# Other engines for the transposes, the squares and the early loads in the first rows of a two-layer image kernel

## The chip, the cores and the metric

The kernel runs on one core of a Trainium2 chip. The metric is the time of one execution on the device, in microseconds (us). In the profile's short names PE is TensorE (PEld its weight loads), DVE is VectorE, ACT is ScalarE, POOL is GpSimd and SP is SyncE, which here only asks for DMAs.

## What is computed

The input is 32 images of 56 x 56 tokens with 128 channels, in fp32. Two residual layers follow one another:

```python
x = x + L0(_gn(x))    # window attention: 7x7 windows, rolled by 3, 4 heads, mask, bias table
x = x + L1(_gn(x))    # DCT along width and along height, 32 modes mixed, inverse DCT, feed-forward
```

`_gn` is a group normalization without weights: 32 groups of 4 channels, mean and variance over the image. In layer 0 each window of 49 tokens makes q, k and v, softmax over 49 keys with a position bias, the product with v and a projection. In layer 1 the first 32 DCT modes of each line are mixed over the channels, once along the width and once along the height, turned back and summed; then comes `relu(h @ W1 + b1) @ W2 + b2` with 512 hidden channels.

## The kernel before

The whole batch is one stream of cycles. A cycle takes in one row of windows (8 windows of 7 x 7 tokens, 392 tokens); an image has 8 such rows, so row r belongs to image r // 8. The work of a row is spread over five cycles, and layer 1 of an image follows from 11 cycles after its first row (`CONV_BEGIN` = 11) over the next 16 cycles. The order on TensorE, ScalarE, VectorE and GpSimd is written out by hand: under `manual_schedule` each of these engines executes its instructions in the order in which the Python code issues them. SyncE's queue is not part of that, and is ordered by the planner.

For row r the stages are:

- cycle r: `attn_q` and `attn_k` (TensorE, evicted by ScalarE), `attn_scores` (TensorE, then VectorE adds the bias and mask, L494), `attn_max` (VectorE takes the maximum, L504, GpSimd subtracts it, L505), `attn_v` (TensorE, copied by ScalarE, L471)
- cycle r or r + 1: `attn_exp` (ScalarE, L511)
- cycle r + 1: `attn_recip` (VectorE sums and inverts, L516 and L518) and `attn_divide` (GpSimd, six multiplications, L530). They write the quotients into `blocks`, cut up in such a way that a transpose of 32 x 32 blocks puts the whole tile right
- cycle r + 2: `attn_transpose` (VectorE, one transpose of 128 x 1024, L540) into `eT`; `load_tokens` asks for the residual input (`xr`)
- cycle r + 3: `add_bias` (GpSimd, L130, on `xr`), `attn_values` (TensorE, output and its bias into `oT` by VectorE, L587, and ScalarE, L589; with the argument `both` by ScalarE alone), `attn_project` (TensorE, then VectorE adds the residual into `x1`, L610; the result is also stored to DRAM)
- cycle r + 4: `attn_sums` (VectorE, L627), `attn_squares` (ScalarE, L639), `sum_squares` (VectorE, L643) and `add_sums` (GpSimd, L653), for the second normalization

Cycles 0 to 10 are written in `first_rows`. Later cycles follow `halves_first`, `eighths`, `quarters`, `behind_max`, `halves_last`. The scratch `a` of the softmax has three buffers in the first cycles and two later; the third is borrowed from a buffer of layer 1 (`xf`).

An image is read in four quarters (`load_quarter`: k is the upper or lower part of the rows, u the left or right half), each with four DMAs of 112 KB, and turned by VectorE (`turn_quarter`, L339 to L344). Image 0's quarters go into the two buffers `y`, which layer 1 first writes in cycle 11. All later images use one buffer `xin`, so a quarter is asked for only when the one before it has been turned. `next_steps` says in which cycle which quarter is turned: for image 1 in cycles 1, 2, 4 and 5, for image 2 from cycle 8 on. `norm_step` issues the first normalization of the next image in pieces.

The constants of layer 1 are asked for by SyncE (`back_weights`: inverse DCT; `ff_weights`: feed-forward), the mixing weights by ScalarE (`mix_weights`). The tag `hid` has four buffers of 128 x 512 for the hidden layer, which begins in cycle 19. TensorE writes into banks `pa0` to `pa3` in turn for the attention (`attn_bank`) and into four banks `pc` for layer 1 (`conv_bank`).

Of the kernel before, what the change touches and what calls it, by code (L numbers as in the profile page):

```python
# [9 lines left out]

F32 = mybir.dt.float32
AF = mybir.ActivationFunctionType
# [30 lines left out]
FF_AT = (8, 9, 10, 12, 13, 14, 15)  # L43
KB = 32
CONV_BEGIN = NWR + 3


@with_exitstack
def swin_fourier_kernel(
# [86 lines left out]

    def load_quarter(b, k, u):

        if b:
            t = work.tile([P, HW, KB], F32, tag="xin", name="xin", bufs=1)  # L140
        elif u:
            t = others[k]
        else:
            t = y_of[k][:, : S * KB].rearrange("p (w c) -> p w c", w=S)
            others.append(t[:, HW:])
            t = t[:, :HW]
        rows = slice(k * (S - KB), k * (S - KB) + KB)
        for cb in range(C // KB):
            cs = slice(cb * KB, (cb + 1) * KB)
            queue = nc.scalar if b == 0 and cb % 2 else nc.sync  # L150
            queue.dma_start(t[cs], x[b, rows, u * HW : (u + 1) * HW, cs])
        return t

    xins, others = {}, []
    for k in range(2):
        for u in range(2):
            xins[0, k, u] = load_quarter(0, k, u)
# [87 lines left out]
    idctw = const.tile([P, 2 * S], F32, tag="idctw", name="idctw")  # L245
    idcth = const.tile([P, S, 2], F32, tag="idcth", name="idcth")

    def back_weights(li):
        if li == 0:
            nc.gpsimd.memset(idctw, 0.0)  # L250
            nc.gpsimd.memset(idcth, 0.0)
        with nc.allow_non_contiguous_dma(reason="constant, once"):
            for blk in range(4 * li, 4 * li + 4):
                ls = slice(blk * NM // 2, (blk + 1) * NM // 2)
                modes = slice(blk // 2 * NM + blk % 2, (blk // 2 + 1) * NM, 2)
                nc.sync.dma_start(idctw[ls], idct_w[modes, li * 2 * S : (li + 1) * 2 * S])
                src = idct_h.rearrange("p (h r) -> p h r", r=4)[modes, :, 2 * li : 2 * li + 2]
                nc.sync.dma_start(idcth[ls, : S - SS], src[:, SS:])
                nc.sync.dma_start(idcth[ls, S - SS :], src[:, :SS])

    w1sb = const.tile([P, NM, C], F32, tag="w1sb", name="w1sb")
    w0sb = const.tile([P, NM, C], F32, tag="w0sb", name="w0sb")
# [10 lines left out]
    b2half = const.tile([P, JP], F32, tag="b2half", name="b2half")  # L273

    def ff_weights():
        nc.sync.dma_start(wff1, W1)
        nc.sync.dma_start(b1sb, b1.rearrange("(f p) -> p f", p=P))
        nc.sync.dma_start(wff2, W2.rearrange("(f p) o -> p f o", p=P))
        nc.sync.dma_start(b2sb, b2.partition_broadcast(P))
        for hs in HALVES:  # L280
            nc.sync.dma_start(b2half[hs], b2[hs].partition_broadcast(JP))

    mhalf = const.tile([P, 1], F32, tag="mhalf", name="mhalf")
    nc.gpsimd.memset(mhalf, -0.5)
# [6 lines left out]

    k_sb = big.tile([P, 2, NWR, WT], F32, tag="k", name="k")
    heads = const.tile([P, 2], F32, tag="heads", name="heads")
    nc.vector.memset(heads, 0.0)
# [2 lines left out]
    q_sb = big.tile([P, RT + JP - WT], F32, tag="q", name="q")  # L299
    nc.gpsimd.memset(q_sb, 0.0)  # L300
    v_sb = [big.tile([P, NP, C], F32, tag=f"v{i}", name=f"v{i}") for i in range(3)]
    a_sb = [big.tile([P, NH, NP, WT], F32, tag=f"a{i}", name=f"a{i}") for i in range(2)]

    def attn_buffer(r):
        return a_sb[r % 3 if r < CONV_BEGIN + 4 else r % 2]

    blocks = [
        big.tile([P, 2, NH * NP, KB], F32, tag=f"blocks{i}", name=f"blocks{i}") for i in range(2)
# [59 lines left out]
    def image_norm(im):  # L368

        GR = C // 16  # L370

        def average(out, src):
            sums = small.tile([P, GR], F32, tag="gsums", name="gsums", bufs=2)
            nc.vector.tensor_reduce(
                sums, src.rearrange("p (g c) -> p g c", c=4), axis=AX.X, op=ALU.add
            )
            nc.vector.tensor_scalar(
                out.rearrange("p (g c) -> p g c", c=4),
                sums.unsqueeze(2).to_broadcast([P, GR, 4]),
                0.25,  # L380
                None,
                ALU.mult,
            )

        nc.vector.bn_aggr(stat[:, 0:2], im.st)

        turned = small.tile([P, 32], F32, tag="turned", name="turned", bufs=2)
        nc.vector.transpose(turned, stat)
        mean = small.tile([P, 2, 32], F32, tag="gmeans", name="gmeans", bufs=1)
        average(mean[:, 0], turned)  # L390
        yield
        nc.vector.tensor_tensor(turned, turned, mean[:, 0], ALU.subtract)
        nc.vector.tensor_tensor(turned, turned, turned, ALU.mult)
        average(mean[:, 1], turned)
        back = small.tile([P, 2, 32], F32, tag="back", name="back", bufs=2)
        nc.vector.transpose(
            back.rearrange("p k c -> p (k c)"), mean.rearrange("p k c -> p (k c)")
        )
        gm = back[:, 0, 0:1]

        im.mean = small.tile([P, 1], F32, tag="mean0", name="mean0")
        nc.vector.tensor_scalar(im.mean, gm, -1.0, None, ALU.mult)

        ve = small.tile([P, 1], F32, tag="ve", name="ve")
        nc.vector.scalar_tensor_tensor(
            out=ve, in0=back[:, 0, 1:2], scalar=1e-5, in1=back[:, 1, 0:1], op0=ALU.add, op1=ALU.add
        )
        rstd = small.tile([P, 1], F32, tag="rstd0", name="rstd0")
        nc.gpsimd.tensor_tensor(rstd, ve, mhalf, ALU.pow)
        im.w = work.tile([P, 3 * C], F32, tag="wn", name="wn")  # L410
        im.bias = small.tile([P, 5], F32, tag="bqkv", name="bqkv")
        yield
        nb = small.tile([P, 1], F32, tag="nb0", name="nb0")
        nc.vector.scalar_tensor_tensor(
            out=nb, in0=gm, scalar=-1.0, in1=rstd, op0=ALU.mult, op1=ALU.mult
        )
        nc.scalar.mul(im.w, wqkv, rstd)  # L417
        yield
        pb = attn_bank()
        halved(pb[:, 0:1], wqkv[:, 2 * C :], nb)  # L420
        nc.vector.tensor_copy(im.bias[:, 2:3], pb[:, 0:1])
        yield
# [97 lines left out]

    def attn_divide(r, rs):
        a3 = attn_buffer(r).rearrange("p t w j -> p (t w) j")
        dst = blocks[r % 2]
        lo, hi = (slice(0, KB), slice(KB, JP)), (slice(JP, JP + KB), slice(JP + KB, P))
        halves = [(slice(0, P), slice(0, P), k, k) for k in range(2)]
        for a, b in (lo, hi):
            halves += [(a, b, 1, 0), (b, a, 0, 1)]
        for to, src, k, kb in halves:
            n = (KB, WT - KB)[kb]
            nc.gpsimd.tensor_tensor(  # L530
                dst[to, k, :, :n],
                a3[src, :, kb * KB : kb * KB + n],
                rs[src].unsqueeze(2).to_broadcast([src.stop - src.start, 2 * NWR, n]),
                ALU.mult,
            )

    def attn_transpose(im, i, r):

        eT = work.tile([P, NH * NP, JP], F32, tag="eT", name="eT")
        nc.vector.transpose(eT.rearrange("p t (k j) -> p k t j", k=2), blocks[r % 2])  # L540
        im.eT[i] = eT

# [91 lines left out]
    def attn_squares(im, i):  # L634
# [1 line left out]
        n0, n1 = WS * i // 2, WS * (i + 1) // 2  # L636
        piece = x1[:, n0:n1]
        im.sq = im.xr.pop(i)[:, : n1 - n0]
        nc.scalar.activation(im.sq, piece, AF.Square, scale=valid)  # L639

    def sum_squares(im, i):

# [331 lines left out]
    def halves_first(cycle):  # L974
# [15 lines left out]
        if im:  # L990
# [2 lines left out]
            attn_k(im, i)  # L993
            if i == NWR - 2:
                wrap_rows(cycle)
        if last and cycle > CONV_BEGIN and not behind_short:
            attn_squares(last, j)
            sum_squares(last, j)
        if not behind_short:
            next_tokens(cycle)  # L1000
        if cycle % NWR == 0:
            norm_step(cycle)
# [50 lines left out]
    def eighths(cycle):  # L1053
        im, i = row(cycle - 3)
        if im:
            attn_values(im, i, cycle - 3, cycle % NWR in VALUES_BY_ACT)
            if cycle % NWR == NWR - 1:
                attn_squares(*row(cycle - 4))
        for im, c in fourier(cycle):
            if c == 0:  # L1060
# [61 lines left out]
    def next_quarter(cycle):  # L1122
        b, quarter, late, _ = next_steps(cycle)
        if quarter:
            turn_quarter(images[b], *quarter)
        if late:
            xins[(b, *late)] = load_quarter(b, *late)

    def wrap_rows(cycle):
# [15 lines left out]

    EARLY = (0, 3, 4, 5, 7)
    VALUES_BY_ACT = (3, 6, 7)

    def halves_last(cycle):
        im, i = row(cycle)  # L1150
# [20 lines left out]
    def next_begin(cycle):  # L1171
        b, quarter, _, _ = next_steps(cycle + 1)
        if quarter:
            if quarter == (0, 0):
                images[b] = image_begin(b)
            xins[(b, *quarter)] = load_quarter(b, *quarter)

    def first_rows(cycle):  # L1180
# [12 lines left out]
        if cycle:  # L1193
            attn_exp(cycle - 1)
        if im3:
            attn_values(im3, i3, cycle - 3)
        tokens_bias(cycle)
        if im:
            attn_scores(im, i, cycle)
# [25 lines left out]
                norm_step(NWR - 1)  # L1225
        if 1 < cycle < 10:
            mix_weights(cycle - 2)
        if cycle in (6, 7):
            back_weights(cycle - 6)
        if cycle == 8:  # L1230
            ff_weights()
        if cycle == CONV_BEGIN - 1:
            attn_sums(im3, i3)
# [5 lines left out]
    with tc.manual_schedule(engines={ET.PE, ET.Activation, ET.DVE, ET.Pool}):  # L1239
        images[0] = image_begin(0)  # L1240
        for k in range(2):
            for u in range(2):
                turn_quarter(images[0], k, u)
            if k:
                copy_wrap(images[0], nc.vector.tensor_copy)
            for i in range(NP * k, NP * k + NP):
                row_stats(images[0], i)
        for _ in range(3):
# [2 lines left out]
            for half in range(2):  # L1251
                bias_and_mask(nc.vector, r, t, half)
        extra = big.tile([P, S, S], F32, tag="xf", name="a_extra", bufs=2)
        extra = extra.rearrange("p r w -> p (r w)")[:, : NH * NP * WT]
        extra = extra.rearrange("p (t w j) -> p t w j", t=NH, w=NP)
        a_sb.append(extra)
        for cycle in range(NB * NWR + CONV_BEGIN + FF_AT[-1] - NWR + 1):
            if cycle < CONV_BEGIN:
                first_rows(cycle)
# [27 lines left out]
                columns_turn(cycle, 0)  # L1287
            columns_turn(cycle, 1)
            last_fetch(cycle)
            if cycle % NWR == NWR - 1 and row(cycle - 4)[0]:  # L1290
                sum_squares(*row(cycle - 4))
                next_tokens(cycle)
            behind_max(cycle)
# [64 lines left out]
```

## Time and profile before

| | |
|---|---|
| time, median of 3 runs | 3254.74 us (3251.01 to 3256.28) |
| the profiled execution | 3245.75 us, its span 3244.0 us |
| TensorE busy | 3136.1 us (97%) |
| VectorE busy | 2538.4 us (78%) |
| GpSimd busy | 2343.1 us (72%) |
| ScalarE busy | 2165.5 us (67%) |
| mean TensorE clock | 0.988 of full |

Busy times are of the whole span. The span can be cut into slices or windows, and each then shows its own share for every engine; matmuls are pipelined and their ends are modelled. A wait is shown beside the instruction that waited, with the instruction that released it. Times in the views count from the start of the span.

### The profile page before, as it was taken

Reading aid. Unit: us, or ns where it says so; the run is one execution under the profiler, and the core shown is the slowest. Engines: PE = TensorE matmul, PEld = TensorE weight load, DVE = VectorE, ACT = ScalarE, POOL = GpSimd, SP = SyncE. Lnnn points to the kernel's source line nnn. Section 1 sums busy time; section 2 is a strip of 40 time slices with the busy share of each in tenths; the row PEclk is TensorE's granted clock in tenths of the full one; section 3 lists DMA queues with packets and bytes.
Section 4 is the critical chain, followed back from the end, with each engine's and each line's share of the span. In section 5 each row is a group of like instructions: output and inputs, shape, how many; then the busy total and the mean of one; then the engine's idle time right before and its main releaser. Section 6 shows DMA issues by size and latency. Waiting matters only on the chain. (4 is left out here: it accounts for less than half of the span.)

```text
span 3244.0 us, 151708 instructions
## 1 busy us (share of the span) xinstructions
PE 3136.1 (97%) x65664; PEld 2363.2 (73%) x65664; DVE 2538.4 (78%) x4787; ACT 2165.5 (67%) x3959; POOL 2343.1 (72%) x2634
## 2 busy tenths in 40 slices
PE   5689999999999999999999999999999999999999
PEld 3467777777777777777777777777777777777776
DVE  8778887878887878888888887878888877887741
ACT  3466776666777666667676776666776666677663
POOL 7777777777777777777777777777777777777741
PEclk8789999999999999999999999999999999999999
DMA  6545556655566656566656556655666656565453
GB/s 113 111 116 147 142 139 145 137 142 139 140 146 146 141 142 144 134 143 148 142 140 147 139 142 145 140 141 144 142 141 148 138 145 144 134 145 139 119 143 96
DMA packets 1173439, 448.46 MB, mean 138 GB/s; under 512 B 529482, under 2 KB 1142908, under 8 KB 1172772
## 3 DMA queue, kind: packets, MB, share of 16 engines
q1 hardware_dynamic: 1163428, 433.22, 56.3%
q8 instruction: 516, 8.45, 1.1%
q10 hardware_dynamic: 8736, 5.38, 0.7%
q14 instruction: 151, 1.24, 0.1%
q0 software_dynamic: 608, 0.17, 0.0%
HBM read 277.00 MB, written 161.48 MB: 135 GB/s over the span
## 5 line engine op out<-in xcount | busy, mean ns | idle before, releaser
L530 POOL TENSOR_TENSOR blocks<-a,rs 128x512 f32<-128x512 f32 x1506 | 1280.0, 857 | 415.1 <-DVE rs L518 291.3
L116 PE MATMUL pc<-xf,wff 128*64 128x512 f32 (+2 forms) x3584 | 714.2, 539 | 1.8 <-DVE xf L820 1.6
L116 PE MATMUL pc<-wff,hid 128*64 128x128 f32 x12288 | 714.1, 273 | 1.7 <-ACT hid L847 1.0
L116 PEld LDWEIGHTS pc<-wff,hid 128*64 128x64 f32 x12288 | 680.4, 137 | 10.3 <-ACT hid L847 5.3
L505 POOL TENSOR_TENSOR a<-a,mx 128x784 f32<-128x784 f32 x251 | 377.7, 1505 | 285.6 <-DVE mx L504 270.2
L116 PEld LDWEIGHTS pc<-xf,wff 128*64 128x64 f32 x3584 | 266.0, 136 | 370.0 <-issue 274.8
L847 ACT ACTIVATE hid<-pc,b1sb 128x512 f32<-128x512 f32 (+2 forms) x896 | 500.5, 643 | 40.9 <-PE pc L116 40.8
L116 PE MATMUL pa<-xw,wn 128*64 128x392 f32 x2048 | 396.0, 501 | 29.8 <-ACT wn L417 29.8
L471 ACT COPY v<-pa 128x512 f32<-128x512 f32 x256 | 151.9, 593 | 349.1 <-PE pa L464 346.2
L494 DVE TENSOR_TENSOR a<-pa,bm 128x392 f32<-128x392 f32 x502 | 260.0, 559 | 152.8 <-PE pa L486 141.6
L451 ACT ACTIVATE k<-pa,bqkv,heads 128x392 f32<-128x392 f32 x512 | 318.9, 674 | 14.7 <-PE pa L116 0.6
L540 DVE STREAM_TRANSPOSE eT<-blocks 128x1024 f32<-128x1024 f32 x256 | 314.2, 1227 | 0.9 <-POOL blocks L530 0.9
L852 POOL TENSOR_TENSOR res<-res,b2sb 128x512 f32<-128x512 f32 (+1 forms) x224 | 252.7, 1128 | 85.1 <-DMA res<-scr 70.8
L438 ACT ACTIVATE q<-pa,bqkv 128x392 f32<-128x392 f32 x256 | 149.8, 585 | 242.6 <-PE pa L116 240.9
L130 POOL TENSOR_TENSOR xr<-xr,bproj 128x384 f32<-128x384 f32 (+1 forms) x256 | 293.0, 1144 | 25.0 <-DMA xr<-in_x_dram 10.5
L738 ACT ACTIVATE y<-modes,rstd 128x448 f32<-128x448 f32 x256 | 276.6, 1137 | 42.9 <-DVE modes L731 31.9
L464 PE MATMUL pa<-wn,xw 128*64 128x128 f32 x4096 | 291.2, 284 | 7.1 <-issue 3.3
L511 ACT ACTIVATE a<-a 128x784 f32<-128x784 f32 x251 | 214.7, 856 | 118.4 <-POOL a L505 118.3
L557 PEld LDWEIGHTS pa<-eT,v 49*32 49x32 f32 x16384 | 173.1, 106 | 161.1 <-issue 63.9
L516 DVE TENSOR_REDUCE sm<-a 128x16 f32<-128x784 f32 x251 | 241.3, 961 | 54.9 <-ACT a L511 54.1
L602 PE MATMUL pa<-wproj,oT 128*64 128x128 f32 x3584 | 246.4, 276 | 20.7 <-DVE oT L587 20.5
L464 PEld LDWEIGHTS pa<-wn,xw 128*64 128x64 f32 x4096 | 227.5, 140 | 45.5 <-ACT oT L589 8.1
(112 smaller groups left out, 4915.1 us busy)
## 6 DMA issues: line engine op xcount, KB each, us to landing
zscr<-z SPq DMA_DIRECT2D x512, 112.0 KB
xin<-in_x_dram SPq DMA_DIRECT2D x496, 112.0 KB
htok<-scr SPq DMA_DIRECT2D x256, 196.0 KB
zT<-zscr SPq DMA_DIRECT2D x192, 256.0 KB
res<-scr SPq DMA_DIRECT2D x160, 256.0 KB
out_dram<-res SPq DMA_DIRECT2D x160, 256.0 KB
scr<-x SPq DMA_DIRECT2D x256, 112.0 KB
xr<-in_x_dram SPq DMA_DIRECT2D x256, 84.0 KB
```

Of the source, the lines that this page charges most:

```text
L116: nc.tensor.matmul(dst[ps], lhsT=lhsT[:, ps], rhs=rhs, start=start, stop=stop)
L130: nc.gpsimd.tensor_tensor(piece, piece, bproj.unsqueeze(1).to_broadcast([P, n, C]), ALU.add)
L451: nc.scalar.activation(k_sb[:, u], pk[:, :RT].rearrange("p (w j) -> p w j", j=WT), AF.Identity, bias=im.bias[:, 3 + u : 4 + u], scale=head ...
L464: nc.tensor.matmul(pv[HALVES[w % 2], w // 2 * C : (w // 2 + 1) * C], lhsT=im.half[i // NP][:, t0 : t0 + JP], rhs=im.w[:, 2 * C : 3 * C], s ...
L494: nc.vector.tensor_tensor(a[:, 2 * hp : 2 * hp + 2, :, 0:WT].rearrange("p u w j -> p w u j"), ps[hp][:, :RT].rearrange("p (w u j) -> p w u ...
L505: nc.gpsimd.tensor_tensor(a3, a3, mx.unsqueeze(2).to_broadcast([P, 2 * NWR, WT]), ALU.subtract)
L530: nc.gpsimd.tensor_tensor(dst[to, k, :, :n], a3[src, :, kb * KB : kb * KB + n], rs[src].unsqueeze(2).to_broadcast([src.stop - src.start, 2 ...
L540: nc.vector.transpose(eT.rearrange("p t (k j) -> p k t j", k=2), blocks[r % 2])
L602: nc.tensor.matmul(pp[hs, (n - n0) * C : (n - n0 + 1) * C], lhsT=oT[:, t0 : t0 + JP], rhs=wproj, start=True, stop=True,)
L738: nc.scalar.mul(y[:, r], t.rearrange("p (n k) -> p n k", k=NM), im.rstd)
L847: nc.scalar.activation(hf[:, :n], ph[:, :n], AF.Relu, bias=b1sb[:, f : f + 1])
L852: nc.gpsimd.tensor_tensor(im.res[:, :k], im.res[:, :k], b2sb.unsqueeze(1).to_broadcast([P, k, C]), ALU.add,)
```

## The change

For the first 16 rows (images 0 and 1) the softmax quotient is formed in place by one GpSimd multiplication, and TensorE transposes it by 32 matmuls against an identity, in two `pc` banks that ScalarE copies into `eT`. The `a` buffers get a tail of 15 zeros so that a 64 column slice of the last window stays inside, and keep their rotation over three until row 17. In `first_rows` the values are evicted by ScalarE alone. The squares of the first 11 rows are made by GpSimd in a `hid` buffer. Image 1's quarters go into the `y` buffers too, each asked for once image 0's quarter there has been turned. The constants of layer 1 are asked for by ScalarE, in smaller portions for the inverse DCT. In all images, squares and token loads of the cycle with i = 6 now stand as late as those of i = 7.

```diff
+TURNED_BY_PE = 2 * NWR
     def load_quarter(b, k, u):
-        if b:
+        if b > 1:
             t = work.tile([P, HW, KB], F32, tag="xin", name="xin", bufs=1)
-        elif u:
-            t = others[k]
         else:
             t = y_of[k][:, : S * KB].rearrange("p (w c) -> p w c", w=S)
-            others.append(t[:, HW:])
-            t = t[:, :HW]
+            t = t[:, u * HW : (u + 1) * HW]
...
-    def back_weights(li):
-        if li == 0:
-            nc.gpsimd.memset(idctw, 0.0)
-            nc.gpsimd.memset(idcth, 0.0)
+    nc.gpsimd.memset(idctw, 0.0)
+    nc.gpsimd.memset(idcth, 0.0)
+
+    def back_weights(blk):
+        li = blk // 4
...
-                nc.sync.dma_start(idctw[ls], idct_w[modes, li * 2 * S : (li + 1) * 2 * S])
...
+            nc.scalar.dma_start(idctw[ls], idct_w[modes, li * 2 * S : (li + 1) * 2 * S])
...
     def ff_weights():
-        nc.sync.dma_start(wff1, W1)
...
+        nc.scalar.dma_start(wff1, W1)
...
+    ident = work.tile([P, HB], F32, tag="hid", name="ident", bufs=NF)[:, :P]
+    make_identity(nc, ident)
...
-        turned = small.tile([P, 32], F32, tag="turned", name="turned", bufs=2)
+        turned = small.tile([P, 32], F32, tag="turned", name="turned", bufs=1)
...
     def attn_divide(r, rs):
         a3 = attn_buffer(r).rearrange("p t w j -> p (t w) j")
+        if r < TURNED_BY_PE:
+            nc.gpsimd.tensor_tensor(
+                a3, a3, rs.unsqueeze(2).to_broadcast([P, 2 * NWR, WT]), ALU.mult
+            )
+            return
...
     def attn_transpose(im, i, r):
         eT = work.tile([P, NH * NP, JP], F32, tag="eT", name="eT")
+        if r < TURNED_BY_PE:
+            a2 = a_ends[r % 3]
+            for g in range(0, NH * NP, NWR):
+                pt = conv_bank()
+                for k in range(NWR):
+                    for u, hs in enumerate(HALVES):
+                        nc.tensor.matmul(
+                            pt[u * JP : (u + 1) * JP, k * WT : (k + 1) * WT],
+                            lhsT=a2[:, (g + k) * WT : (g + k) * WT + JP],
+                            rhs=ident[:, u * JP : u * JP + WT],
+                            start=True,
+                            stop=True,
+                        )
+                nc.scalar.copy(
+                    eT[:, g : g + NWR, :WT], pt[:, :RT].rearrange("p (k j) -> p k j", j=WT)
+                )
+            im.eT[i] = eT
+            return
...
     def attn_squares(im, i):
...
-        nc.scalar.activation(im.sq, piece, AF.Square, scale=valid)
+        if NWR * im.b + i < CONV_BEGIN:
+            im.sq = work.tile([P, HB], F32, tag="hid", name="sq", bufs=NF)
+            im.sq = im.sq.rearrange("p (n c) -> p n c", c=C)[:, : n1 - n0]
+            nc.gpsimd.tensor_tensor(im.sq, piece, piece, ALU.mult)
+        else:
+            nc.scalar.activation(im.sq, piece, AF.Square, scale=valid)
...
     # halves_first
-        if last and cycle > CONV_BEGIN and not behind_short:
+        late = im and i in LATE_SQUARES
+        if last and cycle > CONV_BEGIN and not late:
             attn_squares(last, j)
             sum_squares(last, j)
-        if not behind_short:
+        if not late:
             next_tokens(cycle)
...
     # eighths
-            if cycle % NWR == NWR - 1:
+            if row(cycle)[0] and cycle % NWR in LATE_SQUARES:
                 attn_squares(*row(cycle - 4))
...
+    LATE_SQUARES = (6, 7)
...
     # first_rows
-            attn_values(im3, i3, cycle - 3)
+            attn_values(im3, i3, cycle - 3, True)
...
         if 1 < cycle < 10:
             mix_weights(cycle - 2)
-        if cycle in (6, 7):
-            back_weights(cycle - 6)
-        if cycle == 8:
+            back_weights(cycle - 2)
+        if cycle == 10:
             ff_weights()
...
     # start
             if k:
                 copy_wrap(images[0], nc.vector.tensor_copy)
+            for u in range(2):
+                xins[1, k, u] = load_quarter(1, k, u)
...
     # behind last_fetch(cycle)
-            if cycle % NWR == NWR - 1 and row(cycle - 4)[0]:
+            if row(cycle)[0] and cycle % NWR in LATE_SQUARES:
                 sum_squares(*row(cycle - 4))
                 next_tokens(cycle)
```

## The prediction

> **What bounds the kernel now.** I read the span in slices first, then windows of 50 us, then the waits and the instructions in order of time from 25 to 235 us. The change touches only that stretch, apart from one move of the squares.
>
> ```profile
> PE   5689999999999999999999999999999999999999
> ...
> DVE  8778887878887878888888887878888877887741
> ...
> POOL 7777777777777777777777777777777777777741
> PEclk8789999999999999999999999999999999999999
> ```
>
> TensorE (PE) is full from the fourth slice on; each slice is 81 us. Only the first three have room. By windows:
>
> ```profile
> 50.00:100.00 50.00, 33.47 (x680) 25.08 (x680) 42.80 (x88) 21.57 (x40) 42.33 (x50) 0.77 0.54 124
> 100.00:150.00 50.00, 32.80 (x642) 23.96 (x643) 40.63 (x76) 21.46 (x37) 38.27 (x44) 0.75 0.47 107
> 150.00:200.00 50.00, 35.60 (x784) 27.57 (x780) 40.52 (x73) 31.46 (x60) 34.10 (x39) 0.86 0.54 123
> 200.00:250.00 50.00, 45.17 (x896) 32.16 (x896) 40.17 (x76) 31.44 (x54) 38.25 (x43) 0.90 0.55 123
> 250.00:300.00 50.00, 49.93 (x1098) 38.89 (x1096) 40.21 (x76) 34.07 (x67) 37.54 (x42) 1.00 0.56 141
> ```
>
> The columns are TensorE, its weight loads, VectorE, ScalarE, GpSimd, clock, DMA share, GB/s. From about 220 us TensorE is busy throughout, at full clock: from row 24 to 32, and from 32 to 40, q starts 96.5 us apart, so 12.06 us a cycle. Whatever is won before 220 us should be kept to the end; nothing can be won after it.
>
> In cycles 4 to 10 (56 to 129 us, 10.5 us each) VectorE and GpSimd share the bound. One cycle, row 5:
>
> ```profile
> 67.23 1.02 DVE L494 TENSOR_TENSOR a_extra<-pa,bm 128x392 f32<-128x392 f32 x2
> ...
> 68.28 0.97 DVE L504 TENSOR_REDUCE mx<-a_extra 128x16 f32<-128x784 f32 x1
> ...
> 69.17 0.68 DVE L643 TENSOR_REDUCE part<-xr 128x32 f32<-128x512 f32 x1
> 69.33 1.50 POOL L505 TENSOR_TENSOR a_extra<-a_extra,mx 128x784 f32<-128x784 f32 x1
> 69.76 0.96 DVE L516 TENSOR_REDUCE sm<-a 128x16 f32<-128x784 f32 x1
> ...
> 70.93 1.19 DVE L540 STREAM_TRANSPOSE eT<-blocks 128x1024 f32<-128x1024 f32 x1
> ...
> 71.15 5.34 POOL L530 TENSOR_TENSOR blocks<-a,rs 128x512 f32<-128x512 f32 x6
> ...
> 72.04 0.52 DVE L610 TENSOR_TENSOR x<-pa,xr 128x384 f32<-128x384 f32 x1
> ```
>
> VectorE runs without a gap, and the sum of the squares (L643) follows the maximum at once, because ScalarE had squared long before. TensorE waits for VectorE, which in turn waits for the input:
>
> ```profile
> PE pa L602 <- DVE oT L587: 19.4, 6, 6.3
> DVE xw L339 <- DMA xin<-in_x_dram: 8.4, 2, 5.7
> ```
>
> In cycles 11 to 17 (11.5 us each) a serial loop decides: project add, values, transform, scores, score add, maximum, subtract, exp, sum, reciprocal, next project add. At cycle 12 it runs 0.63, 1.03, 1.87, 1.58, 1.04, 0.97, 1.50, 0.86, 0.97, 0.25: 10.7 us.
>
> **What the Trainium skill says.** (1) "SBUF — State Buffer", Who interferes with whom: a VectorE instruction with two SBUF inputs contends with a GpSimd one that reads SBUF, and the loser blocks fully. The trace agrees: the 128x32 product at L393 took 0.19 us at 21.61 and 1.07 here, under the divide:
>
> ```profile
> 84.61 1.07 DVE L393 TENSOR_TENSOR turned<-turned 128x32 f32<-128x32 f32 x1
> ```
>
> (2) "TensorE: Matmul & The Clock Gate", Part 1: an idle window (about 3.4 us) halves the clock. It agrees: after waits of 4 to 6 us the 32 score matmuls take 1.58 us, otherwise 0.90. (3) "GPSIMD Engine Reference", 3.1: two-input work costs about 2.6 cycles an element. The bias add at L130 gives (1.27-1.00)/128 = 2.1 ns an element. (4) "DMA: Bandwidth & Descriptors", Issuing engines are not separate DMA queues: another issuer saves only issue time. No run here shows that yet; the issues are 0.33 to 0.5 us on either queue.
>
> **The change part by part** (a minus is a gain).
>
> *Image 1 preloaded, 16 DMAs on SP.* The DMA share was 0.74 at 20 to 30 us and 0.01 at 30 to 40. One quarter (0.45 MB) was already there; 1.35 MB more at the 115 GB/s of the first 20 us is 12 us, and the first quarter is used at 39.6. The start I take as 0; if the loads hold up wqkv or the bias table (VectorE begins on it at 23.77, and had 2.2 us to spare before row 0) it is +3. Since xin stays free, image 2's first quarter no longer waits:
>
> ```profile
> 100.80 1.09 DVE L339 STREAM_TRANSPOSE xw<-xin 128x512 f32<-128x512 f32 x1 [5.69 <-DMA xin<-in_x_dram]
> ```
>
> Its last piece was issued at 97.28, behind SP's waits and the first idct constants. That is -5.7. The next quarter is asked for when the first is turned and takes about 7 us; VectorE has 7 us of work there by the sum below, so of 2.7 us I take -2.2.
>
> *Constants on ScalarE.* Three idct DMAs with one of mix_weights in each of cycles 2 to 9, six ff DMAs at cycle 10: 4 x 0.43 = 1.7 us of ScalarE's sequencer ahead of the next q. ScalarE is 43% busy (21.57 of 50), VectorE's stage is longer: 0, or +0.6 a cycle where the cover fails. SP's 24 idct issues (87.8 to 103.8) go; that gain is counted above.
>
> *Cycles 0 to 3.* No squares yet. The divide of row 0 (5.35 us, ending 45.36) held up its transpose, the values and row 3's scores, and xin cost 1.75. Now one product like L505 (1.5 us) ends at 41.6; TensorE transposes at 41.7 to 43.6, copies follow. Carried to row 4's score add: 56.2 for 59.13. **-3.0.**
>
> *The transpose on TensorE.* 32 matmuls with 128x64 weights and 49 columns. The nearest is L464: 16 in 1.09 us, weights in 0.85. So 1.7 to 2.2 us at full clock, up to 3.9 at half (16 took 1.95). Two ScalarE copies of 128x392 at 0.59. In cycles 4 to 10 TensorE then has 7.2 us at full clock a cycle, under VectorE's.
>
> *Cycles 4 to 10 on VectorE.* From score add to the end of project add it took 5.3 us. The transpose goes (-1.1 of issue slot), and the output bias of the values (L587, -0.6). But the squares now stand on GpSimd behind the subtract, and VectorE's sum of squares stands directly behind the maximum: it waits 0.06 + 1.46 (subtract) + 1.14 (1.00 or 1.28, as L130) + 0.05 = 2.7 us. All that VectorE has behind it, the row sum, reciprocal and project add, waits too; GpSimd's product and TensorE's next values wait for those. Net +1.05 a cycle, x7 = **+7.4**; row 7's second squaring in cycle 10 has no maximum to hide in, +1.5. The bounds are -1.7 a cycle, if the wait falls in time that TensorE needs anyway, and +1.3. The norm step (82.62 to 86.84) no longer meets a 5.3 us divide: **-1.8**. Sum to cycle 10: -3.0-5.7-2.2+7.4+1.5-1.8 = **-3.8**.
>
> *Cycles 11 to 18.* In 11 the divide held row 11's subtract from 137.2 to 139.24: -1.7 (-0.2 if v's copy, now behind the transpose, comes first). In 12 that copy stands before the exp: +1.2 (0 to +1.7). In 14, where TensorE is full (8.8 of 10 us), the transpose costs +1.8. In 15 the divide held the subtract, and with it rstd and the new weights: -2.2. The transposes fill gaps of 4 to 6 us, and scores and inverse transforms run warm: five times 0.7, **-3.4**. Sum **-4.3**.
>
> *Late squares at row 6, all images.* VectorE's sum and the load of xr come some 5 us later; the bias add of the next cycle is behind the load on GpSimd, then the divide. TensorE's work covers that (22 us idle in 3000): 0, bounds -3 and +3. New memsets and the identity go into GpSimd's 5 us of waits before 23 us; spare SBUF and shared slots: 0.
>
> Total -3.8 - 4.3 = **-8**: 3245.75 (span 3244.0 and 1.75 around it) becomes 3237.7. The median of the runs is 9.0 above that execution, so 3246.7.
>
> **Rivals.** *A, clearly faster:* the wait on the squares lies in time that TensorE's order takes anyway, and only the shorter work counts: part of 1.7 x 7 = 12 us gained in place of 8.9 lost. Two thirds of that way is -14: about -22 in all, 3233. For it: VectorE and GpSimd were full at 60 to 90 us. Against: VectorE had no gap where it could wait.
>
> *B, slower:* the transposes run at half clock. TensorE's order from scores to scores is then 3.9 + 1.55 (project) + 1.95 (v) + 2.7 (q, k) + 0.6 + 1.58 = 12.3 us against some 10, in half of seven cycles +8; no -3.4; cycles 12 and 14 lose 2 more each, and the xr loads 2: +9 in all, 3264. For it: the clock of 0.75. It decides if the clock between 50 and 150 us stays under 0.77 although TensorE has more to do.
>
> *C, no effect:* the loop of cycles 11 to 17 contains neither divide nor transpose, and gives the lead back: 0, 3255.
>
> **Numbers.** The likeliest 0.40, A 0.25, B 0.25, C 0.10. A measurement here can tell about 0.2% (6.5 us). Of the likeliest, whose terms reach from -17 to +1, 0.26 lies beyond it and 0.14 within. Faster 0.51, same 0.24, slower 0.25. The range goes from A's -27 to B's +9: 3228 to 3264.
>
> **What would show it.** Right: VectorE's L643 waits about 2.7 us on GpSimd in cycles 4 to 10, no wait of 5.7 at L339, subtract right behind maximum in cycles 11 and 15, transposes of 1.7 to 2.2 us, clock over 0.85 from 50 to 150, TensorE full at about 212 us. Wrong: no such wait, or q of row 11 before 120 us (A); a clock under 0.77 (B); a cycle after 250 us that isn't 12.06.

## The result and the profile after

The changed kernel takes **3249.5 us** (median of 20 runs, 3244.9 to 3254.1), the kernel before 3254.5 in the same comparison (20 runs, 3249.4 to 3258.1): ratio 0.9984, interval 0.9978 to 0.9991, so 5 us less where 8 were forecast. The profiled execution took 3248.8 us, its span is 3247.0.

The number came out, but not by the reasons given. Against the profiled execution of before (3245.7, a quick one, 9 us under its median) the steady part, behind row 24, is 5 us shorter and the start is 8 us *longer*: row 24's q (ScalarE's copy of it out of the bank, as all q starts below) is at 290.0 us in place of 281.9.

The page's slices after the change:

```profile
PE   4789999999999999999999999999999999999999
...
DVE  6678888888888888788888887878887878887741
POOL 4457777777777777777777777777777777777741
...
PEclk9899999999999999999999999999999999999999
```

VectorE fell from 8, 7 to 6, 6 in the first two slices and GpSimd from 7, 7 to 4, 4. Their work was taken away, as planned, but TensorE does not fill its slices any earlier. By windows (columns as before: TensorE, weight loads, VectorE, ScalarE, GpSimd, clock, DMA share, GB/s):

```profile
50.00:100.00 50.00, 38.22 (x910) 32.57 (x904) 29.75 (x59) 23.09 (x53) 21.72 (x20) 0.80 0.50 112
100.00:150.00 50.00, 37.49 (x863) 29.05 (x858) 30.77 (x56) 23.92 (x53) 25.38 (x25) 0.83 0.51 114
```

In the first, VectorE's 42.8 us became 29.8, GpSimd's 42.3 became 21.7, and TensorE rose from 33.5 to 38.2 by the transposes. No engine is full, so something waits for something. One cycle in order of time, row 6's VectorE and GpSimd work and ScalarE's next q:

```profile
87.49 0.97 DVE L510 TENSOR_REDUCE mx<-a 128x16 f32<-128x784 f32 x1
88.63 1.51 POOL L511 TENSOR_TENSOR a<-a,mx 128x784 f32<-128x784 f32 x1 [2.92 <-DVE mx L510]
90.09 0.83 POOL L671 TENSOR_TENSOR sq<-x 128x384 f32<-128x384 f32 x1
90.79 0.59 ACT L477 COPY v<-pa 128x512 f32<-128x512 f32 x1 [1.27 <-PE pa L470]
90.80 0.35 ACTq L266 DMA_DIRECT2D w0sb<-in_w_dram  x1
90.95 0.55 DVE L677 TENSOR_REDUCE part<-sq 128x32 f32<-128x384 f32 x1 [2.50 <-POOL sq L671]
91.19 0.44 ACTq L255 DMA_DIRECT2D idctw<-in_idct_w_dram  x1
91.67 0.43 ACTq L257 DMA_DIRECT2D idcth<-in_idct_h_dram  x1
92.14 0.55 ACTq L258 DMA_DIRECT2D idcth<-in_idct_h_dram  x1
92.79 0.59 ACT L444 ACTIVATE q<-pa,bqkv 128x392 f32<-128x392 f32 x1 [1.18 <-PE pa L118]
```

There are two queues here. In such lines a q after the engine's name (ACTq, SPq) marks its sequencer, which asks for DMAs. VectorE stands 2.5 us between maximum (L510) and sum of squares (L677), the wait that was forecast. And ScalarE asks for four constants from 90.80 to 92.69, 1.9 us; q follows at once at 92.79, though the page calls its wait one for TensorE, whose product it is.

The start itself has two new losses. In the first two lines below, VectorE's small mean stands for GpSimd's clearing of the blocks (the same operation takes 0.18 us at 23.53); in the others, the bias add of row 0's tokens waits 14.3 us for their load, the project add 9.1 for the bias add, and TensorE's values 6.7 for the project add:

```profile
20.25 2.58 DVE L383 TENSOR_SCALAR gmeans<-gsums 128x32 f32<-128x32 f32 x1
20.92 1.86 POOL L317 MEMSET blocks<- 128x1024 f32 x2
...
62.05 0.99 POOL L132 TENSOR_TENSOR xr<-xr,bproj 128x384 f32<-128x384 f32 x1 [14.31 <-DMA xr<-in_x_dram]
63.08 0.56 DVE L639 TENSOR_TENSOR x<-pa,xr 128x384 f32<-128x384 f32 x1 [9.11 <-POOL xr L132]
63.78 1.02 PE L586 MATMUL pa<-eT,v 49*32 49x49 f32 x64 [6.67 <-DVE x L639]
```

SP's own waits name the cause: the last loads of image 1, and behind them those of the tokens, stand for loads of the mixing weights (w1sb) that ScalarE asks for only at 46.0 and 55.8 us:

```profile
SPq L150 <- DMA w1sb<-in_w_dram: 23.3, 2, 22.6
...
SPq L126 <- DMA w1sb<-in_w_dram: 6.3, 1, 6.3
```

They share no data with these. SP goes on at 50.9 us, 4.9 us after the first of them was asked for; in e5 below, which asks for it at 42.7, SP goes on at 46.7. (The mixing weights were on ScalarE before the change, too.)

### The profile page after: what moved, and what is told of

Same layout as the page of the kernel before. It is cut to its first block, busy times and chain, and to the rows that moved or that the text cites. A ratio compares the mean times of both kernels' runs of the same rounds, so it can differ in the third digit from the quotient of the medians.

```text
span 3247.0 us, 153715 instructions
## 1 busy us (share of the span) xinstructions
PE 3158.3 (97%) x66688; PEld 2384.5 (73%) x66688; DVE 2516.1 (77%) x4747; ACT 2182.5 (67%) x4004; POOL 2297.8 (71%) x2570
## 3 DMA queue, kind: packets, MB, share of 16 engines
q1 hardware_dynamic: 1154244, 432.48, 55.1%
## 5 line engine op out<-in xcount | busy, mean ns | idle before, releaser
L541 POOL TENSOR_TENSOR blocks<-a,rs 32x272 f32<-32x272 f32 (+3 forms) x1434 | 1219.6, 858 | 389.7 <-DVE rs L524 255.1
L118 PEld LDWEIGHTS pc<-xf,wff 128*64 128x64 f32 x3584 | 262.2, 136 | 373.8 <-issue 272.0
L457 ACT ACTIVATE k<-pa,bqkv,heads 128x392 f32<-128x392 f32 x512 | 318.9, 674 | 14.3 <-PE pa L118 0.4
L569 DVE STREAM_TRANSPOSE eT<-blocks 128x1024 f32<-128x1024 f32 x240 | 295.2, 1230 | 0.0
L470 PE MATMUL pa<-wn,xw 128*64 128x128 f32 x4096 | 284.6, 279 | 4.9 <-issue 3.8
L510 DVE TENSOR_REDUCE mx<-a 128x16 f32<-128x784 f32 x250 | 242.2, 969 | 7.6
```

The lines of the kernel that those rows point to most:

```text
L118: nc.tensor.matmul(dst[ps], lhsT=lhsT[:, ps], rhs=rhs, start=start, stop=stop)
L457: nc.scalar.activation(k_sb[:, u], pk[:, :RT].rearrange("p (w j) -> p w j", j=WT), AF.Identity, bias=im.bias[:, 3 + u : 4 + u], scale=head ...
L470: nc.tensor.matmul(pv[HALVES[w % 2], w // 2 * C : (w // 2 + 1) * C], lhsT=im.half[i // NP][:, t0 : t0 + JP], rhs=im.w[:, 2 * C : 3 * C], s ...
L510: nc.vector.tensor_reduce(mx, a3, axis=AX.X, op=ALU.max)
L541: nc.gpsimd.tensor_tensor(dst[to, k, :, :n], a3[src, :, kb * KB : kb * KB + n], rs[src].unsqueeze(2).to_broadcast([src.stop - src.start, 2 ...
```

## The experiments

Each ran beside the kernel before. The table has the ratio to it with its interval, and from each profile the q starts of rows 4, 5, 11 and 24 (us from the span's begin) and the distance from row 5's to row 11's. How far q runs ahead of VectorE differs from row to row, and cycle 10 has the six feed-forward loads in it; so the last column has a second measure, from VectorE's project add of row 1 to that of row 7 (cycles 4 to 10).

| kernel | ratio | row 4 | 5 | 11 | 24 | 5 to 11 | adds |
|---|---|---|---|---|---|---|---|
| before, as shown | 1 | 55.7 | 62.0 | 128.9 | 281.9 | 66.9 | 63.0 |
| before again (e1) | 0.9999 (0.9991-1.0008) | 56.0 | 62.0 | 129.5 | 285.3 | 67.5 | 63.6 |
| late squares alone (e2) | 0.9976 (0.9969-0.9983) | 56.7 | 63.1 | 131.1 | 286.3 | 67.9 | 64.0 |
| image 1 preloaded alone (e11) | 0.9990 (0.9982-0.9998) | 54.0 | 60.1 | 127.0 | 282.8 | 66.9 | 63.1 |
| **the change** | 0.9984 (0.9978-0.9991) | 57.8 | 73.0 | 136.5 | 290.0 | 63.5 | 62.4 |
| + tokens first (e3) | 0.9968 (0.9956-0.9981) | 58.1 | 66.6 | 130.8 | 283.2 | 64.2 | 62.3 |
| + squares on ScalarE (e4) | 0.9992 (0.9984-1.0000) | 58.6 | 74.0 | 138.5 | 294.9 | 64.5 | 62.6 |
| + issues behind k (e5) | 0.9970 (0.9958-0.9981) | 55.1 | 67.0 | 130.4 | 281.5 | 63.4 | 60.4 |
| + both of these (e6) | 0.9933 (0.9920-0.9945) | 54.0 | 67.1 | 119.6 | 270.1 | 52.5 | 51.4 |
| + constants on SP (e9) | 0.9971 (0.9960-0.9983) | 54.1 | 62.2 | 129.1 | 276.7 | 67.0 | 62.4 |
| all repairs (e7) | 0.9930 (0.9918-0.9943) | 53.1 | 61.2 | 118.1 | 269.8 | 56.8 | 56.1 |
| e7, VectorE transposes (e8) | 0.9949 (0.9936-0.9963) | 51.8 | 58.2 | 117.6 | 269.0 | 59.4 | 55.9 |
| all repairs, constants on SP (e10) | **0.9917** (0.9903-0.9930) | 52.9 | 60.9 | 110.8 | 262.2 | 49.9 | 49.3 |
| e10, VectorE transposes (e12) | 0.9936 (0.9923-0.9950) | 52.6 | 59.0 | 116.4 | 267.4 | 57.4 | 53.8 |

### Before, once more (e1)

No edit.

> The kernel before, unchanged, once more. The profiled execution shown before (3245.75) lies 9 us under the median of its runs, so the 5 us by which the changed kernel is faster can't be read from one pair of profiles. Theory 1: the steady part is the same in every execution (images 96.48 us apart, step from row 6 to 7 of 8.50 us) and the difference between executions lies in a few images that take 1 to 4 us more, all of it waiting of TensorE's sequencer: time ratio 1.000 +- 0.001, rows 0 to 32 at the same places within 1 us. Theory 2: the shown execution had a lucky start: row 32's q comes about 386 us after the span's begin and not 378.4.

Both theories hold in part. Rows 0 to 11 came within 1 us, and images are 96.5 us apart at the least, in the middle 97.2, and up to 99.6; in the longest of them most of the excess is TensorE idle at its own sequencer ("issue" in the waits). Row 32's q was at 381.7, between the two forecasts; the 3.4 us over the first profile arose in small steps between rows 11 and 20. So one pair of profiles resolves the start to some 3 us, no better.

### The late squares alone (e2)

```diff
-        if last and cycle > CONV_BEGIN and not behind_short:
+        if last and cycle > CONV_BEGIN and not late:       # late: rows 6 and 7
...
-            if cycle % NWR == NWR - 1:
+            if row(cycle)[0] and cycle % NWR in LATE_SQUARES:
                 attn_squares(*row(cycle - 4))
...
```

> The kernel before with the late squares alone: in rows 6 of images 2 and later, too, square, sum of squares and the load of the tokens stand behind the scores. Theory 1 (the whole measured gain of 5 us is here): the step from row 6 to row 7 falls from 8.50 to 8.36 us in each of some 29 images, -4 us, ratio 0.9988, the start as before. Theory 2 (as predicted, TensorE covers this): 0, ratio 1.000, and the gain is in the first eighteen rows.

The gain is there: 0.9976, which is 7.8 us (7.1 by the medians), and in the trace the step from row 6 to row 7 is 8.36 us, in before 8.50. What was saved can be read in one line of before's query for L464, the product for v, "its engine sat idle before it", with the time and the count:

```profile
  ACT oT L589: 8.1, 31
```

ScalarE squared (L639, 0.62 us) ahead of its copies of the values (L589), and TensorE's v product waited 0.26 us for these, once an image. With the squares behind the copies that line is gone from the same query, in this kernel and in the changed one. 29 steps of 0.14 make 4.1 us. The other 3.7 of the measured gain are in no step that I could single out, and this execution's span, 3246.6, lies above its kernel's median of 3241.7; that part stays open. By itself this edit is at least as fast as the whole change (0.9984, the intervals overlap): what the change does to the first rows brought no gain that these times show.

### Tokens first (e3)

```diff
-        if im:
+        if im and cycle > 3:
             load_tokens(im, i)
...
+            if k == 0:
+                for i in range(2):
+                    load_tokens(images[0], i)
             for u in range(2):
                 xins[1, k, u] = load_quarter(1, k, u)
```

> The changed kernel, but the token loads of rows 0 and 1 are asked for on SP ahead of the sixteen loads of image 1's quarters. Theory 1 (those loads stand behind image 1's in SP's order and hold up row 4's scores by 9 us, which are never won back): the score add of row 4 moves from 66.3 to about 57 us after the span's begin, row 32's q from 386.4 to about 378, time -8 us against the changed kernel, ratio to before about 0.996. Theory 2 (the later rows wait for GpSimd's squares and ScalarE's issues anyway and the delay is absorbed by row 11): row 11's q moves by less than 2 us and the time by less than 2.

Theory 1. Row 4's score add moved from 66.4 to 60.8, not to 57, row 11's q came 5.7 us earlier and row 32's 6.8 (386.4 to 379.6); the time fell to 0.9968. The delay is not absorbed.

### Squares and issues: each alone, and both (e4, e5, e6)

```diff
 # e4
...
-            nc.gpsimd.tensor_tensor(im.sq, piece, piece, ALU.mult)
+        nc.scalar.activation(im.sq, piece, AF.Square, scale=valid)   # in place, as before
 # e5: the same calls, in first_rows
             attn_values(im3, i3, cycle - 3, True)
+        if 1 < cycle < 10:
+            mix_weights(cycle - 2)
+            back_weights(cycle - 2)
+        if cycle == 10:
+            ff_weights()
 # e6: e5, and ScalarE squares into the spare buffer
```

> The changed kernel with the squares of the first rows on ScalarE again. Theory 1 (VectorE's wait of 2.7 us on GpSimd's squares lengthens each of cycles 4 to 10 by about 1 us, as predicted): the wait goes, row 11's q comes about 7 us earlier after row 4's, the time falls by 6 to 8 us. Theory 2 (the wait lies in time that the order of TensorE or ScalarE takes anyway): the wait goes, the distance from row 4's q to row 11's (78.7 us) changes by less than 2 us and the time by less than 2.

> The changed kernel, with the constants' DMAs asked for by ScalarE behind the output copies of the values (so behind q and k) instead of ahead of the next q; squares still on GpSimd. Theory 1 (two loops of about the same length run side by side in cycles 5 to 10: VectorE waiting for GpSimd's squares, and ScalarE and TensorE in turn, with about 2 us of DMA issues ahead of q): taking the issues out alone leaves the other loop, so the distance from row 5's q to row 11's (63.5 us) falls by 0 to 3 us only. Theory 2 (the issues alone set the pace): it falls by about 2 us a cycle, 10 us or more.

> As the one before, and the squares of the first rows on ScalarE as well, into the same spare buffer that the changed kernel gives to GpSimd's squares (so the token buffer comes free as early). Theory 1 (two loops): now both are shortened, and the distance from row 5's q to row 11's falls from 63.5 to about 55 us, what remains being TensorE's transposes at half clock (3.2 us) and the rest of its order, about 9 us a cycle. Theory 2 (squares alone are free, as the run with squares on ScalarE seemed to show): no more than the kernel with the issues moved alone.

e4: VectorE's wait went, and nothing came of it (64.5 us from row 5 to row 11, where the change has 63.5). By the rule I had set, the wait was free. But the waits between 73 and 125 us, first of e4, then of the changed kernel, show what stood beside it; the columns are the sum, the count and the longest:

```profile
PEld pa L492 <- ACT k L457: 9.3, 5, 2.2
```

```profile
DVE part L677 <- POOL sq L671: 13.1, 5, 2.7
...
PEld pa L492 <- ACT k L457: 3.6, 4, 1.8
```

In e4 TensorE waits for ScalarE's k. The end of one of its cycles:

```profile
91.94 0.59 ACT L477 COPY v<-pa 128x512 f32<-128x512 f32 x1 [1.27 <-PE pa L470]
...
94.19 0.59 ACT L444 ACTIVATE q<-pa,bqkv 128x392 f32<-128x392 f32 x1 [1.43 <-PE pa L586]
```

The cycle from q at 83.92 to q at 94.19 closes without a gap: q and k 1.78, scores 1.17, transposes 3.10, project 0.88, v 1.09, v's copy and the four issues 2.25, together 10.27. That is a second loop, about as long as the one through GpSimd's squares. e5 takes only the second away: 63.4 from row 5 to row 11, nothing again by that mark, and 60.4 by the project adds, in place of 62.4, so 2.0 us. VectorE still stands for the squares in every cycle, and its cycle is 10.1 us long (60.4 over six). e6 takes both: **52.5**, by the project adds 51.4, and 0.9933. Two loops of nearly one length ran side by side, and taking away either left the other. One blemish: e4 squares in the token buffer and so reloads it later (GpSimd waits 12.4 us for tokens in four cycles); spare-buffer squares with the issues ahead of q were not run. In the cycle summed up above, tokens held up nothing of that chain; for the other cycles this is not shown.

e5's time fell by more, to 0.9970: its issues come earlier in a cycle (the second four begin at 49.2 us, not 55.8), SP's token loads no longer wait 6.3 us for a mixing load, and row 5's q comes at 67.0 for 73.0.

### Constants on SP (e9)

```diff
-            nc.scalar.dma_start(idctw[ls], ...)
+            nc.sync.dma_start(idctw[ls], ...)
 # likewise idcth, mix_weights and ff_weights; the same cycles
```

> The changed kernel with the constants (mixing weights, inverse transforms, feed-forward weights) asked for on SP in the same cycles, and nothing else. Theory 1 (SP's queue stands because its loads of image 1 wait for a load that ScalarE asks for only in cycle 2, with which they share no data): the sixteen loads are asked for by about 35 us and not 53, row 4's score add comes 7 us or more earlier (distance from row 4's q to row 5's about 8.5 us in place of 15.1); the distance from row 5's q to row 11's stays near 63.5, since GpSimd's squares still hold VectorE. Theory 2 (the loads are held by the rate of the DMA or by their buffer): SP stands to 50 us as before.

Theory 1 for SP. SP's sixteen loads of image 1, first in the changed kernel, then here (start, duration of the whole group):

```profile
19.17 33.98 SPq L150 DMA_DIRECT2D y<-in_x_dram  x16
```

```profile
19.21 11.26 SPq L150 DMA_DIRECT2D y<-in_x_dram  x16
```

In e9 they are asked for by 30.5 us, and row 5 follows row 4 by 8.1 us in place of 15.1. So the coupling to ScalarE's issues had held them, not the DMA's rate. The other half missed by the mark that I had set: row 5 to row 11 took 67.0, not 63.5. By the project adds it held: 62.4 us, as in the changed kernel, and VectorE's wait for the squares came to 21.6 us in eight waits between 50 and 130, the longest 4.1. Row 5's q, no longer held, ran further ahead of VectorE, and the next rows lost that again (11.9 us to row 6).

### All repairs (e7), and with the constants on SP (e10)

```diff
 # e7 = e3 + e6, and behind the first norm:
         for _ in range(3):
             norm_step(-1)
+        for t in blocks:
+            nc.gpsimd.memset(t, 0.0)
 # e10 = e7, but the issues where the change has them, on nc.sync
```

> All repairs together on the changed kernel: token loads of rows 0 and 1 ahead of image 1's quarters, constants' DMAs behind the values' copies, squares on ScalarE into the spare buffer, and GpSimd's clearing of the two large block buffers behind the first norm. If the losses of the start add up as read from the traces: row 0's q at 26.1 in place of 27.5, row 4's near 56, row 11's near 120, time about 16 us under the changed kernel's, ratio to before 0.994. If a further bound (TensorE at half clock) takes over: row 11's q no earlier than 126, ratio about 0.9965.

> All repairs, but the constants on SP in place of behind the values on ScalarE. Theory 1 (ScalarE's issues couple the two queues, and the six of cycle 10 hold ScalarE for 5 us): no wait of SP on a constant, cycle 10 shorter by about 3 us, row 11's q at about 112 and not 118; time 4 to 6 us under the kernel with all repairs. Theory 2 (SP's order then delays image 2's quarters and the tokens, as it did in the kernel before): xin or xr waits of 3 us or more in cycles 6 to 10, row 11's q at 118 or later, time equal.

e7 gives 0.9930. Row 0's q came at 25.6, 2.0 us earlier (e3 and e6, which leave the clearing where it was, have 27.5 and 27.7), so the clearing was the cause of that loss. But what e7 has ahead of e6 at row 5 (5.8 us) is down to 1.5 at row 11, and the times are equal. Most of it goes from row 6 to row 7, which takes 12.7 us and in e6 8.4: SP's loads of tokens stand 4.1 us for a mixing load (w1sb) that ScalarE asks for at 62.6, and GpSimd waits for the tokens:

```profile
70.35 0.99 POOL L132 TENSOR_TENSOR xr<-xr,bproj 128x384 f32<-128x384 f32 x1 [8.76 <-DMA xr<-in_x_dram]
```

In cycle 10 the six feed-forward loads, in e6 as in e7, stand in ScalarE's order ahead of a square for which VectorE waits; in e7 they take from 108.50 to 113.44:

```profile
113.49 0.61 ACT L669 ACTIVATE sq<-x,valid 128x384 f32<-128x384 f32 x1 [4.00 <-issue]
```

With the constants on SP (e10) both go: row 6 to row 7 takes 8.1 us for 12.7, row 10 to row 11 9.5 for 12.5, row 11's q is at 110.8 (112 was expected), and the time is **3220.8 us, 0.9917**, the best here. No wait of SP on a constant is left; GpSimd still waits up to 4.3 us for tokens.

### TensorE's transposes taken back (e8, e12)

```diff
-        if r < TURNED_BY_PE:
+        if r < 0:                      # in attn_divide and attn_transpose
```

> The same with the transposes of the first sixteen rows on VectorE again, and with them the division that writes the blocks on GpSimd (5.3 us a row); a third attention buffer and all else as in the kernel with all repairs. Theory 1 (TensorE's transposes shorten the first rows): rows 4 to 11 take longer here, about 10.5 us a cycle, and the clock between 50 and 150 us is lower; 5 to 10 us slower than with all repairs. Theory 2 (at half clock a transpose of 3.2 us costs TensorE's loop as much as it saves VectorE and GpSimd): within 2 us of it, or faster.

> The kernel with all repairs and the constants on SP, with the transposes of the first sixteen rows on VectorE again and the division that writes the blocks on GpSimd (5.3 us a row). With the constants behind the values on ScalarE, row 24's q came at the same place with and without TensorE's transposes (269.0 and 269.8). Theory 1 (there both met the issues of cycle 10; without them TensorE's transposes do shorten the rows): the distance from row 5's q to row 10's is 40.5 us with them and about 45 without; row 24's q at 266 to 269 in place of 262.2, time 4 to 7 us more. Theory 2 (a transpose of 3.2 us at half clock costs TensorE's loop what it saves VectorE and GpSimd): within 2 us.

e8 is inconclusive: row 24's q is where e7's is, yet its median is 4 us higher, with intervals that overlap. e12 speaks for theory 1: row 5 to row 10 takes 46.1 us in place of 40.5, row 24's q is 5.1 us later, the time 3227.3 for 3220.8. The intervals of the ratios touch here, too (by 0.0007), but all five executions of e12 (from 3226.4 on) lie above all four of e10 (up to 3224.8), and the trace agrees. The windows of 50 to 100 us, first of e10, then of e12:

```profile
50.00:100.00 50.00, 42.47 (x1245) 34.81 (x1241) 42.43 (x81) 35.57 (x79) 25.60 (x23) 1.00 0.54 125
```

```profile
50.00:100.00 50.00, 33.83 (x754) 25.03 (x754) 45.35 (x82) 27.97 (x60) 45.63 (x52) 0.84 0.47 110
```

With the transposes on TensorE the clock is 1.00 and GpSimd has half its time free; without them VectorE and GpSimd are both over 90%. So TensorE's transposes, together with the division in place that they allow, are worth some 6 us, once nothing else holds the rows; the two were not taken apart.

### Image 1 preloaded alone (e11)

```diff
 # on the kernel before
...
+            for u in range(2):
+                xins[1, k, u] = load_quarter(1, k, u)
```

> The kernel before with image 1's quarters loaded behind image 0's and nothing else (divide, VectorE transposes, squares on ScalarE, constants on SP in cycles 2 to 8 as before). Theory 1 (as predicted: the waits of 5.7 and 2.7 us for image 2's and 1's quarters go, and nothing takes their place): row 11's q at about 121 to 123 in place of 129, ratio 0.9975. Theory 2 (another wait of SP or VectorE takes their place): row 11's q within 2 us of 129, ratio 1.000.

Between the two: row 11's q came 2.0 to 2.6 us earlier, ratio 0.9990. SP stood 15.9 us for the mixing weights here, too, and where image 2's first quarter had cost 5.7 us its second now cost 7.2:

```profile
DVE xw L336 <- DMA xin<-in_x_dram: 7.2, 1, 7.2
```

## Why the prediction was right in number and wrong in reason

That -5 came near -8 was luck: the start was forecast 8 us shorter and came out longer, and the gain came where 0 was forecast.

**Late squares, 0 (-3 to +3).** This is the step that failed to the good: 4.1 us by the steps, 7.8 by the time of e2. I asked whether TensorE's work covers later squares, and not whether ScalarE's earlier square delayed something in before. The line with 31 waits on oT was in the profile; that nothing can be won behind 220 us was wrong.

**The first eighteen rows, -8.** They came out 5 to 8 us longer (row 24: 290.0 against 285.3 and 281.9). Its terms:

- *Start 0 (bound +3):* +1.5. Not the preload, but "new memsets 0": both of GpSimd's clearings of the blocks now stand behind its wait for the bias table, in VectorE's norm, where before one did. The Trainium skill ("SBUF — State Buffer", Who interferes with whom) counts tensor_scalar among the operations that can take the port shared with GpSimd, and says that the one that comes second is blocked fully. The trace agrees as to the block: 2.58 us for 0.18, ending with the memsets (at 22.83 and 22.78). That VectorE came second it does not show: the record of its operation begins at 20.25, that of the first of these memsets at 20.45.
- *Cycles 0 to 3, -3.0:* row 4's score add at 66.4, not 56.2. The step assumed row 0's tokens to be there. The DMAs of the preload were counted, but not what is behind them in SP's order. e3 and e9 show this, at 6 to 7 us.
- *Reloads, -5.7 and -2.2:* VectorE's waits for image 2's quarters did go (1.3 us in all from 20 to 240 us). Alone the preload brings 2 to 2.6 us at row 11 (e11), as new waits take their place.
- *Constants on ScalarE, 0 or +0.6 a cycle:* mis-sized in kind. ScalarE was judged by its busy share (43%), but it lies in series with TensorE: each microsecond of issue ahead of q is one of the loop. With the squares' wait gone, moving the issues saved up to 1.9 us a cycle (project adds, 62.6 in e4 and 51.4 in e6, over six cycles; the squares' buffer differs, too). The skill's sentence that another issuer saves only issue time ("DMA: Bandwidth & Descriptors", Issuing engines are not separate DMA queues) fits an issue (0.35 to 0.55 us on ScalarE, in before 0.33 to 0.54 on SP for most), but the issue time had been moved to the costlier place, and the two queues were coupled besides.
- *VectorE net +1.05 x 7:* the wait was 2.5 to 2.7 us, as forecast (2.7), and the squares took 0.83 and 1.04 us for 1.00 and 1.28. Its price was shared: taken away alone it gives nothing (e4), together with the issues 11 us from row 5 to row 11 (e6 against the change).
- *The transposes, 1.7 to 2.2 us, up to 3.9:* 2.07 at full clock and up to 3.65, but by two errors that cancel: there are 64 instructions a row, not 32, at 32 ns each and not 60.
- *Norm step -1.8:* right (94.19 to 96.67, 2.5 us in place of 4.2).
- *Warm clock -3.4, over 0.85 from 50 to 150 us:* missed, 0.80 and 0.83. In e10 it is 1.00 from 50 to 100 us, with the same transposes and fewer waits: they are not what kept it low. The reading of before behind this term was loose: there the scores took 1.58 us after waits of 2.8 and 3.4 us, too, not only of 4 to 6.
- *Cycles 11 to 18, -4.3 in all:* not seen. From row 11's q to row 24's it was 153.0 and 155.8 us in the two profiles of before, and 153.6 after.

**The rivals.** B's mechanism, transposes at half clock, was there (2.9 to 3.65 us in rows 1 to 7), but not as the cause: in e10 five of these seven take 2.07. A was right that the squares' wait lies beside other time, and wrong that time would be gained. C was right that cycles 11 to 17 bring nothing, but there was no lead for them to give back. The -27 at which the range begins was not worked out: A's own sum is -22. Of the signs, the waits at L677 and the lost wait at L345 came; subtract behind maximum came in cycles 11 and 15 (0.1 us between them); TensorE full at 212 us did not: from 222 to 232 it is busy 7.6 of 10. A sign against it came: behind 250 us the shortest images take 96.34 us, 12.04 a cycle and not 12.06, which is the late squares.

The balance closes to about 5 us only. A start that is 5 to 8 us longer and a steady part that is 5 to 7 shorter, by the two profiles of before, do not add up to -5; medians of 20 runs say -5.0, and single executions scatter by as much.

## What to carry to other kernels

Remove suspects in pairs: where two loops run side by side at one length, each alone looks nearly free (0 and 2 us here), and both together were worth 11 us. Judge an issue or a copy by the loop that it stands in, not by its engine's busy share, and for every DMA that is put early ask what stands behind it on its queue. Measure a stretch between marks on the engine that sets its pace. An edit in the steady loop of 0.14 us an image can outweigh a rebuilt start.

## What was not expected of the hardware

A queue that only asks for data stood 23 us for a load on another engine's queue with which it shares no data; with all on one queue the same sixteen loads were asked for in 11.3 us in place of 34.0. By what the two are tied was not tried. DMA issues on ScalarE took 0.35 to 0.55 us each for the most part, but up to 2.3 in e7's cycle 10. And images take up to 2 to 4 us more than the shortest of the same execution (96.34 us in the changed kernel, 96.5 in before), mostly with TensorE idle at its own sequencer: 23 us in all over 28 images in the changed kernel, 24 and 26 in before. Why it waits there is not known.
